# Layer 0 of a four-layer network as Strassen's seven products over both batch halves, with the input taken in four parts

## The chip, the cores and the metric

The kernel runs on one core of one Trainium2 chip. A core has a matrix engine (TensorE, PE in the profile), three engines for elementwise work (VectorE or DVE, ScalarE or ACT, GpSimd or POOL), and SyncE (SP), which here issues nearly all transfers between DRAM and the on-chip memory (SBUF). Matmul results land in PSUM, eight banks of 128 x 512 fp32, and another engine has to copy or add them out. The metric is device time in microseconds; lower is better. Every number is fp32 unless a tile is marked bf16.

## The reference

Four residual layers on a batch of 1024 images of 16 x 16 x 16. Ahead of each layer the activations are normalised in groups. Layer 0 is a tensor-train matrix of three cores; written out it is a dense 4096 x 4096 matrix applied to each image. Layers 1 and 3 are a neural cellular automaton (two depthwise convolutions, two dense layers, a mask), and layer 2 is a 3 x 3 convolution.

```python
def _L0_conv_ref(vector, core0, core1, core2):
    # IN_DIMS = OUT_DIMS = [16, 16, 16], RANKS = [1, 16, 16, 1], BATCH = 1024
    for core in cores:
        r, o, i, k = core.shape
        res_t = res.reshape(bs, r, i, -1)
        new = jnp.einsum('roik,brix->bkox', core, res_t)
        ...
    return res.reshape(bs0, *out_dims)
```

The tuned kernel doesn't apply the three cores one after another. It multiplies the cores into the 4096 x 4096 matrix on the chip, tile by tile, and multiplies that with the normalised activations. For each layer the result is x + layer(normalise(x)).

## The kernel before: the parts that matter

The batch is split into two chunks (n = 0, 1) of 512 images. `XN[n]` holds the normalised activations of one chunk in SBUF, 32 lines of 128 partitions x 512 images; `xf[l][n]` is the residual stream in DRAM. While TensorE works on one chunk, the other engines load and normalise the other one in the background.

The input is loaded with images on partitions, turned by TensorE, copied to `XN`, stored back to DRAM in the new order, and then normalised there with sums over all 32 lines:

```python
def input_steps(X, n):
    ...
    def turn(h, j, wh, xs):
        pt = psum([P, 4, P], "ptin")
        for bg in range(4):
            T.transpose(pt[:, bg], xs[bg][:, j, 8 * wh : 8 * wh + 8]..., ident)
        evac(X[:, 16 * wh + h + j], pt.rearrange("p g b -> p (g b)"))   # ACT and DVE in turn
    ...                                    # then 16 stores rows_in(xf[0][n], w) <- X

def norm_lines(X, gm, on_act=True):
    # sum over lines (DVE), mean over groups (one matmul with gm), subtract,
    # squares (ACT) and their sum (DVE), one matmul, rsqrt by Newton, multiply
    ...
```

Layer 0 is 32 output tiles x 32 input tiles for each chunk. The weight tiles of an output tile are built in two halves (`build`): eight matmuls of 16 rows, two to each of four 32-row groups of TensorE, into four PSUM banks, each copied to SBUF. For chunk 0 they are built and also saved to `w_dram`; for chunk 1 they are read back:

```python
def layer_train(X, n):
    ...
    def build(i, ih):
        wload(i, ih)                                   # the SBUF tile
        pw = [bank([P, 2, S, S], "w", "pw") for _ in range(4)]
        for v in range(2):
            for r in range(4):
                T.matmul(pw[r][:, v], g[32 * r : 32 * r + 16, ...], st["c0"][32 * r : 32 * r + 16],
                         start=True, stop=True)
        for r in range(4):
            evac(w[:, :, r].rearrange("p i v o -> p v i o"), pw[r])
        nc.sync.dma_start(w_dram[i, ih], ...)
    ...
    def piece(i, k):                                   # 32 output tiles x 8 pieces of 4 matmuls
        def go():
            if k == 0:
                st["po"] = bank([P, NB], "o", "po0")   # two banks
            for j in range(4 * k, 4 * k + 4):
                ih, i1 = divmod(j, S)
                T.matmul(po, st["w", i, ih][:, i1]..., X[:, 16 * ih + i1], start=j == 0, stop=j == NL - 1)   # L818
            prepare(i + 1, k)                          # build (n = 0) or load (n = 1) the next tile's weights
            if k == 0 and i + 1 < NL:
                fetch(i + 1)                           # the residual, 256 KB
            if k == 7:
                V.tensor_tensor(r, r, po, ALU.add)     # L827
                nc.sync.dma_start(tile_cw(xf[1][n], i), r)
```

The order of the program, up to the second layer:

```python
train_setup(X1)                                        # multiply cores 1 and 2 together, to g_dram
for step in input_steps(X0, 0) + norm_lines(X0, gm_in): ...   # chunk 0, nothing beside it
...
run(layer_train(X0, 0), (),
    [conv weights] + make1 + make3                     # weights of layers 1, 2 and 3
    + input_steps(X1, 1) + norm_lines(X1, gm_in))      # chunk 1, in the background
run(layer_train(X1, 1), [put(L1)] + load_cw(X0, xf[1][0]), norm_cw(X0, True), 0.2, by=0.15)
run(layer_nca(X0, 0, 1, L1), load_cw(X1, xf[1][1]), norm_cw(X1, False), 0.2, by=0.3)
```

`make1` and `make3` prepare the weights of the two automaton layers; their `fold` steps are matmuls of 9 x 36 x 512 (L370) whose results go to DRAM.

Of the kernel before, what the change touches and what calls it, by code (L numbers as in the profile page):

```python
# [9 lines left out]
F32 = mybir.dt.float32  # L10
# [5 lines left out]
ORDERED = {ENG.PE, ENG.DVE, ENG.Activation, ENG.Pool}  # L16
# [9 lines left out]
ALIVE = 0.1  # L26

# [72 lines left out]
def conv_preact_kernel(ctx: ExitStack, tc: tile.TileContext, a: dict, out: bass.AP):  # L100
# [15 lines left out]

    pool = {}
# [34 lines left out]
    def cst(name, shape, dt=F32):  # L152
# [3 lines left out]
    gind = cst("gind", [P, 2, 8])  # L156
    gm_in = cst("gm_in", [P, 8, 8, 2])
    V.tensor_reduce(gind[:, 0], ident.rearrange("p (w g i) -> p g w i", g=8, i=2), AX.XY, ALU.add)
    V.tensor_scalar(
        gm_in, gind[:, 0].unsqueeze(1).unsqueeze(3).broadcast_to([P, 8, 8, 2]), 1.0 / 512, None,  # L160
        ALU.mult,
    )
    gm_in = gm_in.rearrange("p w g i -> p (w g i)")
    gm_wc = cst("gm_wc", [P, 4, 8, 4])
    V.tensor_reduce(gind[:, 1], ident.rearrange("p (w g i) -> p g w i", g=8, i=4), AX.XY, ALU.add)
    V.tensor_scalar(
        gm_wc, gind[:, 1].unsqueeze(1).unsqueeze(3).broadcast_to([P, 4, 8, 4]), 1.0 / 512, None,
# [51 lines left out]
    def nca_weights(pre, room):  # L219
# [130 lines left out]
        def fold(n):  # L350
            def go():
                for f in range(2):

                    uses = []
                    for m, pats in enumerate(TRIPLES):
                        for i, pat in enumerate(pats):
                            over = m == 2 and i > 0 or m == 3 and i > 1
                            if over == bool(f):
                                for v in range(2):
                                    if pat[v] == n:  # L360
                                        ks = range(3) if m < 2 else [m - 2]
                                        uses += zip(ks, slots(m, i), [v] * 3)
                    if not uses:
                        continue
                    e = fold_e[f]
                    for a2 in range(2):
                        pe = psum([P, NB], pre + "pe")
                        for hh in range(2):
                            h0 = NB * (2 * hh + a2)
                            T.matmul(  # L370
                                pe[64 * hh : 64 * hh + 36], tp[:, n, f], fs[:, h0 : h0 + NB],
                                start=True, stop=True,
                            )
                        for hh in range(2):
                            rows = slice(64 * hh, 64 * hh + 36)
                            evac(e[rows, NB * a2 : NB * a2 + NB], pe[rows])
                    for k, s, v in uses:
                        for hh in range(2):
                            r0 = 64 * hh + 12 * k
                            nc.sync.dma_start(  # L380
                                wy.rearrange("q g v h s k -> v s (q g) h k")[
                                    v, s, :, 8 * hh : 8 * hh + 8
                                ],
                                e[r0 : r0 + 12].rearrange("p (h k) -> p h k", h=8),
                            )

            return go

        steps = [inputs, 8, dense0, 4, bias_lines, 4, bias_rows, dense1, xpats, taps, 8, order, 4]
        return L, steps + [x for n in range(len(TERMS)) for x in (fold(n), 10)]  # L390


# [44 lines left out]
    g_dram = dram.tile([S, 16, S, 256], F32, tag="g_dram", name="g_dram")  # L437
    w_dram = dram.tile([NL, 2, P, 16 * P], F32, tag="w_dram", name="w_dram")
    c_dram = dram.tile([16, 256], F32, tag="c_dram", name="c_dram")

    def train_setup(room):

        flat = room.rearrange("p n b -> p (n b)")
        c0 = flat[0:16, 14336:14592].rearrange("p (i o) -> p i o", o=S)
        c0n = flat[:, 0:32].rearrange("p (t k) -> p t k", t=2)
        c2 = flat[0:16, 512:768]
        c1n = flat[:, 1024:1536].rearrange("p (t f) -> p t f", t=2)
# [9 lines left out]
        c1t = flat[0:16, 2048:6144].rearrange("p (t i m) -> p t i m", t=2, i=S)  # L457
        for t in range(2):
            for i2 in range(0, S, 4):
                pt = psum([16, 4, P], "pc1")  # L460
                for j in range(4):
                    T.transpose(pt[:, j], c1n[:, t, 16 * (i2 + j) : 16 * (i2 + j) + 16], ident)
                evac(c1t[:, t, i2 : i2 + 4], pt)
        for t in range(2):

            g = flat[:, 6144 + 4096 * t : 10240 + 4096 * t].rearrange("p (o j i) -> p o j i", o=S, j=S)
            for i2 in range(0, S, 2):
                pg = psum([P, 2, S, S], "pg")
                for j in range(2):
                    T.matmul(pg[:, j], c1t[:, t, i2 + j], c2, start=True, stop=True)  # L470
                evac(g[:, :, i2 : i2 + 2, :].rearrange("p o j i -> p j o i"), pg)
            nc.sync.dma_start(
                g_dram[:, 8 * t : 8 * t + 8].rearrange("o k q f -> (k q) o f"),
                g.rearrange("p o j i -> p o (j i)"),
            )
        pt = psum([16, 2, P], "pc0")
        for t in range(2):
            T.transpose(pt[:, t], c0n[:, t], ident)
        for t in range(2):
            evac(  # L480
                c0[:, :, 8 * t : 8 * t + 8].rearrange("p i o -> p o i"),
                pt[:, t].rearrange("p (o i) -> p o i", i=S),
            )
        nc.sync.dma_start(c_dram, c0.rearrange("p i o -> p (i o)"))
# [70 lines left out]
    def rstd(st):  # L555


        def root():
            st["t"] = work([P, NB], "s", "t")
            A.activation(st["t"], st["ve"], AF.Sqrt)  # L560

        def newton():
            ve, t = st["ve"], st["t"]
            r = st["r"] = work([P, NB], "n", "r")
# [8 lines left out]
    def norm_lines(X, gm, on_act=True):  # L573
# [5 lines left out]
        def mean():  # L579
            st["p"] = psum([P, NB], "pmean")  # L580
            T.matmul(st["p"], gm, s1["s"], start=True, stop=True)

        def var():
            st["v"] = psum([P, NB], "pvar")
            T.matmul(st["v"], gm, s2["s"], start=True, stop=True)
# [9 lines left out]
    def norm_cw(X, on_act):  # L595


        st = {}
        sums, sq, mean, var, keep, spread = [], [], [], [], [], []
        for q in range(4):  # L600
# [4 lines left out]
            sums.append(more1)  # L605
            sq.append(each(X, l0, 8, lambda q=q: st["m", q], ALU.subtract) + more2)
# [13 lines left out]
            def keep_q(rows=rows):  # L620
                if rows.start == 0:
# [7 lines left out]
            mean.append(mean_q)  # L629
            var.append(var_q)  # L630
            keep.append(keep_q)
            spread.append(spread_q)
        steps = sums[0] + woven(sums[1], (2, mean[0]), (3, held(st, 0))) + [1] + sq[0]
        for q in (1, 2):
            steps += woven(
                sums[q + 1], (2, var[q - 1]), (3, mean[q]), (4, keep[q - 1]), (4, held(st, q))
# [3 lines left out]
        steps += woven(sq[2][4:], (2, mean[3]), (3, held(st, 3)))  # L640
        steps += woven(sq[3], (2, var[2]), (4, keep[2])) + [5, var[3], 2, keep[3]]
        steps += rstd(st) + [4, spread[0], 2, held(st, 0), 2]
        for q in range(4):
            mul = each(X, 8 * q, 8, lambda q=q: st["m", q], ALU.mult)
            steps += woven(mul, (2, spread[q + 1]), (3, held(st, q + 1))) if q < 3 else mul
# [32 lines left out]
    def input_steps(X, n):  # L678

        steps = []  # L680

        def load(h, xs):
            for bg in range(4):
                b0 = n * NB + bg * P
                x = work([P, 4, S, C], "xi", "xin")
                nc.sync.dma_start(
                    x.rearrange("p h w c -> p (h w c)"),
                    a["x"][b0 : b0 + P, h : h + 4].rearrange("b h w c -> b (h w c)"),
                )
                xs.append(x)  # L690

        def turn(h, j, wh, xs):
            pt = psum([P, 4, P], "ptin")
            for bg in range(4):
                T.transpose(  # L695
                    pt[:, bg], xs[bg][:, j, 8 * wh : 8 * wh + 8].rearrange("p w c -> p (w c)"), ident
                )
            evac(X[:, 16 * wh + h + j], pt.rearrange("p g b -> p (g b)"))

        for h in range(0, S, 4):  # L700
            xs = []
            steps += [lambda h=h, xs=xs: load(h, xs), 8]
            for j in range(4):
                for wh in range(2):
                    steps.append(lambda h=h, j=j, wh=wh, xs=xs: turn(h, j, wh, xs))
        for w in range(S):
            steps.append(
                lambda w=w: nc.sync.dma_start(  # L708
                    rows_in(xf[0][n], w),
                    X[16 * (w % 8) : 16 * (w % 8) + 16, 16 * (w // 8) : 16 * (w // 8) + 16],  # L710
                )
            )
# [515 lines left out]
```

## Time and profile before

| | |
|---|---|
| time, median of 3 | 3480.26 us (3471.43 to 3483.19) |
| span of the profiled execution | 3475.3 us |
| granted TensorE clock, mean | 0.968 |
| start to first product of layer 0 | 158.3 us |
| layer 0, chunk 0 and chunk 1 | 158.3 to 2102.9 us |
| moved by DMA | 441.76 MB, mean 127 GB/s |

How to read it: section 1 of the page gives each engine's busy time; section 2 cuts the span in 40 slices of about 87 us and prints the busy share of each in tenths. The chain that ended last is followed back from the final instruction, at each step to whatever released it; its shares by line say what the time was spent on. Groups of instructions are named by kernel line, engine, operation and tiles (L818 is the product of layer 0), with count, busy time and mean duration, and the idle time before them with its releaser. A matmul of this kernel leaves two records, and the ends of matmuls are modelled, so distances from start to start are used for its cost. A timeline lists instructions by start time and duration.

### The profile page before, as it was taken

The numbers are of one execution on the slowest core, as the hardware profiler recorded it, in microseconds if no ns is written. First come the engines' busy times: TensorE is split into PE (matmuls) and PEld (weight loads), VectorE is DVE, ScalarE is ACT, GpSimd is POOL, SyncE is SP. The second block draws the span as 40 slices with busy tenths as digits, with TensorE's granted clock in tenths as the row PEclk, the third lists the DMA queues.
The fourth block names the chain that finished last, engine by engine and source line by source line (L and its number), as shares of the span: only waits on it lengthen the run. The fifth ranks groups of instructions, "written<-read, shape, count | busy, mean of one in ns | idle before, by whom it ended". The sixth has DMA issues, their size and how long they took to land.

```text
span 3475.3 us, 35747 instructions
## 1 busy us (share of the span) xinstructions
PE 3310.1 (95%) x14298; PEld 1362.7 (39%) x14298; DVE 1272.4 (37%) x1400; ACT 883.6 (25%) x1370; POOL 420.1 (12%) x314
## 2 busy tenths in 40 slices
PE   5299999999999999999999999999999999999996
PEld 4144444444544444444444443333332333333332
DVE  5611111111135300111110013856777775855322
ACT  2201110111102000000000005666661115665553
POOL 0000000000000000000000002533550002532221
PEclk6599999999999999999999999999999999999998
DMA  8224323323382243222223224445446545442455
GB/s 227 68 89 121 100 88 109 99 89 139 137 181 94 102 157 115 103 91 91 91 91 106 93 76 159 131 129 174 139 127 229 197 157 174 131 130 80 140 148 182
DMA packets 202262, 441.76 MB, mean 127 GB/s; under 512 B 31986, under 2 KB 88222, under 8 KB 184158
## 3 DMA queue, kind: packets, MB, share of 16 engines
q1 hardware_dynamic: 202096, 439.47, 39.4%
q8 instruction: 113, 1.85, 0.2%
q14 instruction: 53, 0.43, 0.0%
HBM read 253.52 MB, written 174.19 MB: 123 GB/s over the span
## 4 chain that ended last, share of the span: by engine, by line
PE 84%; issue 5%; POOL 4%; DVE 3%; DMA 1%; SPq 1%; ACT 0%; POOLq 0%; DVEq 0%; ACTq 0%
PE po L818 51%; PE ph L1109 13%; PE po L962 5%; PE po L857 5%; PE po L877 2%; POOL res L1012 2%; PE pw L775 2%; POOL u L1011 2%; PE L_conv_pe L370 1%; DVE s L503 1%; DVE xn L532 1%; PE ptin L695 1%; PE pg L470 1%; SPq L708 1%; PE ptout L730 1%
## 5 line engine op out<-in xcount | busy, mean ns | idle before, releaser
L818 PE MATMUL po<-xn,w 128*128 128x512 f32 x4096 | 1801.2, 599 | 6.5 <-DMA w<-w_dram 6.5
L818 PEld LDWEIGHTS po<-xn,w 128*128 128x128 f32 x4096 | 775.7, 191 | 989.4 <-issue 989.3
L1112 ACT ACTIVATE hid<-ph,pack 128x512 f32<-128x512 f32 x1024 | 654.3, 687 | 459.2 <-PE ph L1109 332.8
L1109 PE MATMUL ph<-xn,wq 32*128 32x512 f32 x3664 | 574.0, 614 | 0.5 <-DMA wq<-L_conv_wy 0.5
L1011 POOL TENSOR_TENSOR u<-u,mask 128x512 f32<-128x512 f32 x128 | 195.8, 1530 | 2451.2 <-DMA nx<-xn 1573.9
L827 DVE TENSOR_TENSOR res<-res,po 128x512 f32<-128x512 f32 x64 | 44.0, 688 | 1002.6 <-PE po L818 1002.5
L1109 PEld LDWEIGHTS ph<-xn,wq 32*128 32x128 f32 x3664 | 229.2, 185 | 267.1 <-issue 237.1
L1109 PE MATMUL ph<-xn,pack 32*128 32x512 f32 x1288 | 297.0, 626 | 1.2 <-ACT hid L1112 0.9
L962 PE MATMUL po<-hid,pack 128*32 128x512 f32 x2048 | 280.2, 606 | 0.0
L532 DVE TENSOR_TENSOR xn<-xn,m 128x1024 f32<-128x1024 f32 x192 | 258.4, 1400 | 58.9 <-ACT m L543 41.6
L144 ACT COPY w<-pw 128x512 f32<-128x512 f32 x128 | 68.7, 589 | 713.0 <-PE pw L775 361.6
L146 DVE COPY w<-pw 128x512 f32<-128x512 f32 x128 | 82.5, 686 | 407.6 <-PE pw L775 313.6
L1012 POOL TENSOR_TENSOR res<-res,u 128x512 f32<-128x512 f32 x128 | 212.7, 1662 | 16.4 <-DMA res<-xf 6.7
L857 PE MATMUL po<-xn,convw 128*128 128x512 f32 x368 | 170.8, 608 | 8.3 <-DMA convw<-conv_dram 8.3
L974 DVE SCALAR_TENSOR_TENSOR u<-po,pack,xn 128x512 f32<-128x512 f32 x128 | 95.9, 749 | 178.4 <-PE po L962 174.9
L503 DVE TENSOR_TENSOR sq<-sq 128x1024 f32<-128x1024 f32 x108 | 146.6, 1358 | 24.2 <-ACT sq L517 19.6
L543 ACT COPY m<-pmean 128x512 f32<-128x512 f32 x20 | 11.7, 585 | 555.9 <-PE pmean L611 480.8
L1109 PEld LDWEIGHTS ph<-xn,pack 32*128 32x128 f32 x1288 | 113.0, 187 | 97.3 <-issue 66.7
L517 ACT ACTIVATE sq<-xn 128x1024 f32<-128x1024 f32 x80 | 84.5, 1057 | 253.2 <-DVE sq L503 185.9
L503 DVE TENSOR_TENSOR s<-s,xn 128x1024 f32<-128x1024 f32 x88 | 121.7, 1383 | 2.9
L962 PEld LDWEIGHTS po<-hid,pack 128*32 128x32 f32 x2048 | 42.4, 108 | 183.5 <-issue 134.9
L857 PEld LDWEIGHTS po<-xn,convw 128*128 128x128 f32 x368 | 67.3, 191 | 110.3 <-issue 93.8
(120 smaller groups left out, 1376.5 us busy)
## 6 DMA issues: line engine op xcount, KB each, us to landing
w_dram<-w SPq DMA_DIRECT2D x64, 1024.0 KB
res<-xf SPq DMA_DIRECT2D x256, 256.0 KB
w<-w_dram SPq DMA_DIRECT2D x64, 1024.0 KB
xf<-res SPq DMA_DIRECT2D x224, 256.0 KB
xn<-xf SPq DMA_DIRECT2D x96, 512.0 KB
wq<-L_conv_wy SPq DMA_DIRECT2D x192, 192.0 KB
xin<-in_x_dram SPq DMA_DIRECT2D x32, 512.0 KB
xf<-xn SPq DMA_DIRECT2D x32, 512.0 KB
```

The source lines that it names most:

```text
L146: V.tensor_copy(dst, src)
L503: return lambda: V.tensor_tensor(st["t"], st["t"], p(), ALU.add)
L517: A.activation(q, X[:, l : l + 2], AF.Square)
L532: V.tensor_tensor(part, part, m().unsqueeze(1).broadcast_to([P, 2, NB]), op)
L818: T.matmul(po, st["w", i, ih][:, i1].rearrange("p c v o -> p (c v o)"), X[:, 16 * ih + i1], start=j == 0, stop=j == NL - 1,)
L857: T.matmul(st["po", h][wh], conv["fw"][:, y], X[:, 16 * wh + h + y - 1], start=y == ys[0], stop=y == ys[-1],)
L962: T.matmul(po[32 * j : 32 * j + 32], nca["w1"][:, v], hid[j], start=v == 0, stop=v == 1)
L974: V.scalar_tensor_tensor(u, po, nca["b1"], X[:, 8 * q + w2], ALU.add, ALU.add)
L1011: G.tensor_tensor(u, u, st["m"][:, w2], ALU.mult)
L1012: G.tensor_tensor(r, r, u, ALU.add)
L1109: T.matmul(ph, w, x, start=k == 0, stop=k == len(tiles) - 1)
L1112: A.activation(h, ph, AF.Relu, bias=nca["bt"][:, r : r + 1])
```

## The change

Layer 0 is now one pass over both chunks. The two halves of the output (a2), two halves of a part of the input (b) and the two chunks (n) form 2 x 2 block matrices, and Strassen's scheme makes their product with seven block products in place of eight. The combinations of weights come for nothing extra in the weight build (core 0 is combined first, in `R`); those of activations are made by VectorE in place or in `E`; each product is added to or subtracted from one or two output blocks. The SBUF doesn't hold both chunks, so the input comes in four parts of 1024 values, and the output blocks are carried through DRAM from part to part. The first part is split further (phase 0: two products that need chunk 0 alone, phase 1: the other five), so that work starts while chunk 1 is being loaded.

```diff
+    PRODUCTS = [   # weight terms by output half, activation block, where the product goes
+        ({1: {0: 1, 1: 1}}, (0, 0), {(1, 0): 1, (1, 1): -1}),
+        ({1: {1: 1}}, (1, 0), {(0, 0): 1, (1, 0): 1}),
+        ({0: {0: 1, 1: 1}}, (1, 1), {(0, 1): 1, (0, 0): -1}),
+        ({0: {0: 1}}, (0, 1), {(0, 1): 1, (1, 1): 1}),
+        ({0: {0: 1}, 1: {1: 1}}, 0, {(0, 0): 1, (1, 1): 1}),
+        ({0: {0: -1}, 1: {0: 1}}, 1, {(1, 1): 1}),
+        ({0: {1: 1}, 1: {1: -1}}, 2, {(0, 0): 1}),
+    ]
...
+    def layer_train():
+        phases = [(0, 0, 2), (0, 2, 7), (1, 0, 7), (2, 0, 7), (3, 0, 7)]      # part, products from, to
+        units = [(ph, q, w) for ph in range(5) for q in range(4) for w in range(4)]
...
+        def build(u, v):
+            w, n = st["w", u], 4 * (m1 - m0)
+            pw = [bank([P, n, S], "w", "pw") for _ in range(4)]
             for r in range(4):
+                rows = slice(32 * r, 32 * r + 32)
+                T.matmul(pw[r], st["g", u][rows, v], st["R"][rows, p % 2, 64 * m0 : 64 * m1],
+                         start=True, stop=True)
+            for r in range(4):
+                A.copy(w[:, 0:n, 32 * r + 16 * v : 32 * r + 16 * v + 16], pw[r])
...
+        def piece(u, k):                                       # product k of unit u
+                po = bank([P, NB], "o", "po0")                 # three banks now
+                for t in range(4):
+                    x = E[:, what, t] if isinstance(what, int) else X[:, what[0], t, what[1]]
+                    T.matmul(po, st["w", u][:, 4 * k + t], x, start=t == 0, stop=t == 3)
+                if k == 0:
+                    build(u + 1, 0)
+                    if u > 0:
+                        store(u - 1)
+                if k == min(2, m1 - m0 - 1):
+                    build(u + 1, 1)
+                    gload(u + 2)
...                                                            # and fetch(u + 1); residual(u) at k = 1
+                gather(u, k, po, goes)                         # phase 0: A.copy; else V.tensor_tensor, one or two
```

The input's statistics are taken per image, before the turn, where a group's values lie along one partition; mean and 1/sigma are then turned to `mr`, and a part is normalised as it is loaded:

```diff
+        def stats(half, bg):
+            x = slots[:, 4 * half + bg].rearrange("p (q g i) -> p q g i", g=8, i=2)
+            for g in range(8):
+                V.bn_stats(st["b"][:, bg, g, half], x[:, :, g])
...
+        def turn(h, wh):      # as before, but evacuated by ACT alone; part 0 to SBUF, the rest by
+            ...               # three two-line buffers to xr[n] in DRAM
...
+    def part_steps(p):
+        steps = load_part(p) + [10] + normed(p, 0) + normed(p, 1)
+        return steps + combined(p, True) + combined(p, False)
```

The setup of the weights now works in `cores` and four `gs` steps that take their staging tile from the two `r` buffers, one of which holds the cores; each step ends with eight stores of 16 x 16 pieces of 512 bytes to `g_dram`. The order of SyncE is the program's throughout (`ENG.SP` in `ORDERED`). The new program order:

```diff
+        now(loads); now(setup); now(halves[0] + halves[1] + tail)       # shortened
+        start()
+        now(normed(0, 0, 1) + combined(0, True))
+        run(phases[0], bg: chunk 1's loads, statistics and turns, normed(0, 1), combined(0, False))
+        run(phases[1], bg: conv weights + make1 + make3 + part_steps(1))
+        for i in (2, 3):
+            run(phases[i], bg: part_steps(i))
+        run(phases[4] in four quarters, bg: statistics of the quarter before, scaling of quarters 0 to 2)
...
+        run(layer_nca(X0, 0, 1, L1), load_cw(X1, xf[1][1]), (last, 0.0, 0.18),
+            (norm_cw(X1, False), 0.21, 1.0), by=0.3)
```

In phase 4 the results of chunk 0 are gathered in `XN[0]` itself, where layer 1 reads them, so chunk 0 isn't loaded again; `last` is the normalisation of its last quarter, which layer 1 needs later than the others. `make1` and `make3` are cut into shorter steps, with one spare PSUM bank (m = 1) in place of two.

## The prediction

> **What bounds the kernel now.** I read the page's busy shares and its 40 slices first, then the chain that ended last, then the timeline of the first 160 us, and last the timeline of TensorE alone inside layer 0.
>
> ```profile
> PE 3310.1 (95%) x14298; PEld 1362.7 (39%) x14298; DVE 1272.4 (37%) x1400; ACT 883.6 (25%) x1370; POOL 420.1 (12%) x314
> ...
> PE   5299999999999999999999999999999999999996
> ...
> PE 84%; issue 5%; POOL 4%; DVE 3%; DMA 1%; SPq 1%; ACT 0%; POOLq 0%; DVEq 0%; ACTq 0%
> PE po L818 51%; PE ph L1109 13%; PE po L962 5%; PE po L857 5%; PE po L877 2%; POOL res L1012 2%; PE pw L775 2%; POOL u L1011 2%; PE L_conv_pe L370 1%; DVE s L503 1%; DVE xn L532 1%; PE ptin L695 1%; PE pg L470 1%; SPq L708 1%; PE ptout L730 1%
> ...
> L818 PE MATMUL po<-xn,w 128*128 128x512 f32 x4096 | 1801.2, 599 | 6.5 <-DMA w<-w_dram 6.5
> ```
>
> TensorE is full in every slice but the first two and the last, and half of the chain is one line: the products of layer 0 (L818). VectorE and ScalarE are below 40%. So outside the first two slices a microsecond off TensorE is a microsecond off the span, until another engine passes it.
>
> ```profile
> 2.27 9.08 SPq L686 DMA_DIRECT2D xin<-in_x_dram  x12
> ...
> 50.53 40.47 SPq L708 DMA_DIRECT2D xf<-xn  x16
> ...
> 52.29 17.96 DVE L503 TENSOR_TENSOR s<-s,xn 128x1024 f32<-128x1024 f32 x14
> ...
> 97.49 9.17 DVE L532 TENSOR_TENSOR xn<-xn,m 128x1024 f32<-128x1024 f32 x8 [11.00 <-DMA c<-c_dram]
> 106.58 19.83 DVE L503 TENSOR_TENSOR sq<-sq 128x1024 f32<-128x1024 f32 x15
> ...
> 136.78 18.26 DVE L532 TENSOR_TENSOR xn<-xn,r 128x1024 f32<-128x1024 f32 x16
> ...
> 158.28 5.64 PE L818 MATMUL po<-xn,w 128*128 128x512 f32 x8
> ```
>
> This is the start: load, then a serial chain of VectorE passes over the whole chunk (sum, subtract, squares, scale) with a store of 40.5 us in its middle. Layer 0 starts at 158.3 us.
>
> ```profile
> 304.19 1.15 PE L775 MATMUL pw<-c,gq 16*128 16x256 f32 x16
> 305.27 1.91 PE L370 MATMUL L_conv_pe<-xn 9*36 9x512 f32 x8
> 307.11 14.00 PE L818 MATMUL po<-xn,w 128*128 128x512 f32 x32
> 321.04 1.15 PE L775 MATMUL pw<-c,gq 16*128 16x256 f32 x16
> 322.11 7.13 PE L818 MATMUL po<-xn,w 128*128 128x512 f32 x16
> ```
>
> Columns are start and duration in us; the count is in records, two to a matmul (4096 records for the 2048 matmuls of L818). From start to start, 32 records take 321.04 - 307.11 = 13.93 us, so a matmul takes 0.87 us; where the granted clock is 1.00 (1812 to 1943 us: 304 records in 130.35 us) it is 0.86 us, which I use. A build of weights (8 matmuls, 16 records) occupies 1.08 us, a fold of the next layers' weights (4 matmuls) 1.84 us. Layer 0 runs from 158.3 to 2102.9 us, 1944.6 us: chunk 0 up to 1202 us with the builds in it (1044 us), chunk 1 895 us.
>
> **What the Trainium skill says.** (1) "TensorE: Matmul & The Clock Gate", Part 3: matmuls on different 32-row groups run at the same time. The trace agrees: the 8 build matmuls sit on four row groups; by columns each should take half of a 512-column matmul, 0.43 us, together 3.4 us, and they take 1.08. (2) "TensorEngine Tiling (Array Packing)", section PSUM Bottleneck: tiling does not speed up the emptying of PSUM. Agreed here: the bank copies L144 and L146 take 0.59 and 0.69 us, longer than their matmuls. (3) "DMA: Bandwidth & Descriptors", section Queues, rings and completion order: descriptors of a ring are consumed in ring order. The trace fits: the load of c issued behind the 16 stores holds VectorE until 97.5 us. (4) "TensorE: Matmul & The Clock Gate", Part 1: an idle TensorE falls to half clock; the windows from 60 to 160 us show 0.50. No page that I use states the cost of the new per-image statistics instruction.
>
> **The change part by part.**
>
> *Products.* Before, 32 output tiles x 32 input tiles x 2 chunks = 2048 matmuls. After, the 4096 inputs come in 4 parts; in each part 16 units make 7 products of 4 matmuls: 4 x 16 x 7 x 4 = 1792. 256 fewer x 0.86 = -220 us. They are on TensorE, which sets the end.
>
> *Building weights.* Before 64 builds x 1.08 = 69 us, once, kept in DRAM for chunk 1. After, 80 units x 2 builds = 160, and nothing kept. A build is 4 matmuls, one to a row group, with 448 columns for 7 products, 320 for 5 (phase 1), 128 for 2 (phase 0). If the four run together, the streaming is 0.86 x 448/512 = 0.75 us, 0.54 and 0.22; the old build has two rounds of 256 columns = 0.86 and takes 1.08, so a fixed 0.22 comes on top: 0.97, 0.76, 0.44. 96 x 0.97 + 32 x 0.76 + 32 x 0.44 = 93 + 24 + 14 = 131 us, +62.
>
> *Saved and reloaded weights.* 64 MB written and 64 MB read go, and with them the one wait at the chunk boundary, 6.5 us. In their place partial results travel (1 MB in and 1 MB out per unit of 26 us, plus 0.5 MB residual): about 100 GB/s, where the kernel before moves 127. Hidden.
>
> *Gathering.* 12 VectorE additions per unit of seven products x 0.69 us (L827) + one of 1.22 = 9.5 us in 26. The old kernel had 0.69 per 31 us. Normalising the next part adds 26 operations x 1.22 = 32 us per phase of 16 units. VectorE is then near 45%, with three PSUM banks between it and TensorE. ScalarE: 8 copies of 448 columns per unit, about 5 us in 26. Both off the path.
>
> *The start.* Loads as before (8 MB; the window from 10 to 20 us shows 397 GB/s), done near 25 us. Weight setup is now in four stages that share one free staging tile: each waits until the previous one's 1 MB has reached DRAM. With the coefficient tables' trip to DRAM ahead of them, stage stores start near 28 us and each takes about 10 us: the last stage is copied out of PSUM at about 60 us. VectorE is in order, so the 64 statistics instructions (256 elements, estimated at half of the 0.69 us of a 512-column copy: 0.35) run from 61 to 83 us. ScalarE copies 32 transposed lines (0.59 each) from 61 us, but three buffers tie it to the 8 MB of stores, which at 210 to 300 GB/s end near 100 us. Square root, Newton steps on 32 values, widening, transposes and copies: 8 us. Then 8 normalising operations and 2 combining ones x 1.22 = 12 us, of which the first product needs four. First product about 108 us, flow from about 112: against 158.3 that is -46 us.
>
> *New waits inside layer 0.* Phase 0 has to load, transpose and store chunk 1 within some 145 us (16 x (8 x 0.86 + 0.88) + 18 for the transposes), and its small weight loads queue behind 8 MB at about 390 GB/s, 22 us: I allow 12 us. Phase 1 (about 350 us) takes all weight preparation of layers 1 and 3 that was spread over 1044 us; waits of TensorE for small transfers (30 tap loads took 10.3 us to issue, 22 filter loads 16.3) and for the single spare PSUM bank: I allow 18 us. Four phase starts x 2.5 = 10 us. Together +40 us.
>
> *Moved.* The last quarter of the next normalisation goes into the NCA layer: three matmuls, 2.6 us, from one place of TensorE to another. Transposes of inputs are as many as before; the sums' matmuls of the input go (2), 16 small transposes come.
>
> Sum: 3480 - 220 + 62 - 6 - 46 + 40 = 3310 us, a gain of 170 (4.9%).
>
> **The rivals.** *A: the evacuation becomes the bound.* If VectorE or ScalarE falls behind, the three banks fill and TensorE stops at each product. For it: 12 additions in place of one, ordered engines, background operations of 1.22 us in bursts. Against it: 1.4 us of additions per product of 3.44 us. If every product lost 0.3 us, 448 x 0.3 = 134 us and the gain is gone: about 3440. *B: the builds do not overlap or their evacuation stalls TensorE.* If the 4 wide matmuls ran one after another, 160 builds would cost 96 x 3 + 32 x 2.2 + 32 x 0.9 = 387 us rather than 131: slower, about 3565. Against: the old build shows four groups at once; the new rows are at the same multiples of 32. *C: the transfers.* The manual order of SyncE means one store that waits holds the weight loads behind it. In phases 2 to 4 the loads are asked for more than a unit (26 us) ahead, which hides it; in phases 0 and 1 units last 8 and 19 us. At the worst 60 us more: 3370. *D: the start gains nothing*, when setup and statistics queue up in series to 150 us: 3350. *E: everything is hidden*, no new waits and start at 95 us: 3255.
>
> **Range and chances.** Products and builds are counted and timed, 10 us either way. The start carries 20, the waits 35. Range 3250 to 3380. Under 3411 us is faster by over 2%: that takes more than 100 us of waits beyond mine to miss: 0.91. Within 2%: 0.06. Slower: 0.03, rival B or a standstill in the queue.
>
> **What would show it.** Right: product records 3584, still 0.43 us apart; build records in runs of 8 lasting about 1.0 us at 28 tiles; first product near 110 us; phases 2, 3 and 4 about 16 x 26.0 = 416 us each (phase 4 some 10 more); VectorE busy by 40 to 50% there. Wrong: idle gaps of TensorE at every product (A), builds of 3 us (B), gaps released by weight loads or partial results in phases 0 and 1 (C), first product at 140 us or later (D).

## The result, and the profile after

The changed kernel takes 3389.62 us (median of 4, 3388.17 to 3390.83) against 3478.73 us (median of 4, one execution more than in the table above): a ratio of 0.9746, 95% interval 0.9728 to 0.9764. It is faster by 2.5%; 3310 us was predicted, with a range up to 3380.

From the page of the changed kernel, the lines that answer to those shown of before:

```profile
PE 3202.2 (94%) x14050; PEld 1270.3 (37%) x14050; DVE 1636.2 (48%) x2124; ACT 1066.5 (31%) x1944; POOL 420.0 (12%) x314
...
PE   5888797999999999999999999999999999999996
...
PEclk6999898999999999999999999999999999999998
...
L1026 PE MATMUL po<-xn,w 128*128 128x512 f32 x3584 | 1615.5, 606 | 15.9 <-ACT w L973 8.5
...
L968 PE MATMUL pw<-R,gq 32*128 32x448 f32 (+2 forms) x1280 | 143.9, 516 | 8.2 <-DMA gq<-g_dram 8.2
...
L371 PE MATMUL L_conv_pe<-xn 9*36 9x512 f32 x176 | 50.5, 652 | 50.8 <-DMA L_conv_wy<-xn 14.7
```

The products (L1026 now) are 3584 records, as counted. New are the slices 2 to 7 of the TensorE row: they read 8 8 8 7 9 7 where the old kernel had nines from the third on, and the clock row under them has eights. The fold matmuls (L371), 50.5 us of work, have as much idle time in front of them; before, it was 2.3 us. Two lines of before (the clock row, and the folds in the view of groups from 158 to 1170 us):

```profile
PEclk6599999999999999999999999999999999999998
...
L370 PE MATMUL L_conv_pe<-xn 9*36 9x512 f32 x176 | 45.9, 641 | 2.3 <-DVE xn L146 1.1 <-ACT xn L144 1.1
```

Where the 86 us between the two spans (3475.3 and 3388.9 us) come from, by the times at which stages start in the two timelines:

| stage | before | after | difference |
|---|---|---|---|
| start to first product | 158.3 | 93.6 | -64.7 |
| layer 0 | 1944.5 | 1911.1 | -33.4 |
| layers 1 to 3 | 1372.5 | 1384.2 | +11.7 |

Layer 0 by phases is 183.2, 450.4, 427.0, 421.7 and 428.9 us. Each engine's busy time in phases 0 to 4, in this order (columns: the stretch, its length, then busy time and records of each engine, granted clock, DMA share and GB/s):

```profile
93.60:276.80 183.20, 155.12 (x649) 71.95 (x649) 53.69 (x135) 59.71 (x195) 0.00 (x0) 0.97 0.39 144
276.80:727.20 450.40, 386.94 (x1097) 144.93 (x1097) 136.02 (x213) 79.90 (x192) 11.12 (x52) 0.91 0.34 96
727.20:1154.10 426.90, 423.74 (x1152) 178.13 (x1153) 187.08 (x248) 58.87 (x128) 0.00 (x0) 1.00 0.34 114
1154.10:1575.80 421.70, 421.70 (x1153) 177.59 (x1152) 173.56 (x234) 58.87 (x128) 0.00 (x0) 1.00 0.35 115
1575.80:2004.20 428.40, 428.40 (x1154) 179.04 (x1153) 183.45 (x248) 70.73 (x139) 0.00 (x0) 1.00 0.25 82
```

In phase 3 TensorE sets the pace: it is busy in all of its 421.7 us at full clock. Phase 1 makes five products per unit, not seven, and is longer than phase 3. TensorE is idle for 63 us of it, and its mean clock is 0.91. A clock of 0.5 or 1 with a mean of 0.91 over 450 us is half clock for some 81 us; the stretches of the trace at 0.50 add up to 85. What TensorE waited for in phase 1 (the view of waits; us in total, times, longest):

```profile
PE L_conv_pe L371 <- DMA L_conv_wy<-xn: 14.7, 1, 14.7
PE L_conv_pe L371 <- DMA xf<-r: 13.9, 1, 13.9
PE L_conv_pe L371 <- ACT xn L150: 13.0, 7, 3.0
PE L_conv_pe L371 <- DVE xn L152: 9.2, 6, 2.4
PE pw L968 <- DMA gq<-g_dram: 8.2, 1, 8.2
```

Two kinds stand out. Three long waits on transfers, two ahead of the first fold of a layer and one for a unit's weights, make 36.8 us. Thirteen short ones on copies out of PSUM make 22.2 us. One of the short ones, in the timeline (start, duration):

```profile
444.09 1.05 PE L371 MATMUL L_conv_pe<-xn 9*36 9x512 f32 x4
...
445.19 0.68 DVE L152 COPY xn<-L_conv_pe 36x512 f32<-36x512 f32 x1 [0.46 <-PE L_conv_pe L371]
445.95 0.58 ACT L150 COPY xn<-L_conv_pe 36x512 f32<-36x512 f32 x1 [0.36 <-ACT w L973]
446.58 1.05 PE L371 MATMUL L_conv_pe<-xn 9*36 9x512 f32 x4 [1.44 <-ACT xn L150]
```

Half a fold fills the only spare PSUM bank; the second half can't begin until VectorE and ScalarE have emptied it, one after the other. The Trainium skill says as much in "Trainium Kernel Development and Optimization", section Best Practices: regular bubbles can mean that a memory ran out. Here it is PSUM, and the bubbles are 1.4 us.

### The profile page after: what moved, and what is told of

Read it like the earlier page. It is cut to its first block, busy times and chain, and to the rows that moved or that the text cites. A ratio compares the mean times of both kernels' runs of the same rounds, so it can differ in the third digit from the quotient of the medians.

```text
span 3388.9 us, 37017 instructions
## 1 busy us (share of the span) xinstructions
PE 3202.2 (94%) x14050; PEld 1270.3 (37%) x14050; DVE 1636.2 (48%) x2124; ACT 1066.5 (31%) x1944; POOL 420.0 (12%) x314
## 4 chain that ended last, share of the span: by engine, by line
PE 68%; issue 7%; POOL 6%; DVE 2%; SPq 1%; DMA 1%; ACT 0%; POOLq 0%; DVEq 0%; ACTq 0%
PE po L1026 38%; PE ph L1351 12%; PE po L1099 5%; PE po L1204 4%; PE pw L968 3%; POOL res L1254 3%; POOL u L1253 3%; PE po L1119 2%; PE ptout L917 1%; PE L_conv_pe L371 1%; DVE xn L861 0%; PE ptx L1263 0%; PE pmean L670 0%; PE pvar L674 0%; DVE xn L152 0%
## 5 line engine op out<-in xcount | busy, mean ns | idle before, releaser
L1026 PE MATMUL po<-xn,w 128*128 128x512 f32 x3584 | 1615.5, 606 | 15.9 <-ACT w L973 8.5
L1026 PEld LDWEIGHTS po<-xn,w 128*128 128x128 f32 x3584 | 676.0, 193 | 910.0 <-issue 822.8
L1059 DVE TENSOR_TENSOR r<-r,po 128x512 f32<-128x512 f32 x576 | 378.1, 684 | 801.9 <-PE po L1026 725.0
L973 ACT COPY w<-pw 128x448 f32<-128x448 f32 (+2 forms) x640 | 246.8, 471 | 1356.6 <-PE pw L968 1356.0
L591 DVE TENSOR_TENSOR xn<-xn,m 128x1024 f32<-128x1024 f32 x160 | 222.3, 1438 | 30.6 <-ACT m L602 30.6
L1216 DVE SCALAR_TENSOR_TENSOR u<-po,pack,xn 128x512 f32<-128x512 f32 x128 | 95.8, 749 | 169.0 <-PE po L1204 161.6
L1351 PEld LDWEIGHTS ph<-xn,pack 32*128 32x128 f32 x1288 | 113.9, 187 | 103.2 <-issue 63.5
L968 PE MATMUL pw<-R,gq 32*128 32x448 f32 (+2 forms) x1280 | 143.9, 516 | 8.2 <-DMA gq<-g_dram 8.2
L1059 DVE TENSOR_TENSOR xn<-xn,po 128x512 f32<-128x512 f32 x96 | 64.4, 685 | 145.2 <-PE po L1026 145.2
L562 DVE TENSOR_TENSOR sq<-sq 128x1024 f32<-128x1024 f32 x78 | 109.8, 1407 | 15.4 <-ACT sq L576 12.3
L968 PEld LDWEIGHTS pw<-R,gq 32*128 32x128 f32 x1280 | 51.7, 185 | 128.6 <-issue 116.0
L371 PE MATMUL L_conv_pe<-xn 9*36 9x512 f32 x176 | 50.5, 652 | 50.8 <-DMA L_conv_wy<-xn 14.7
```

The lines of the kernel that those rows point to most:

```text
L562: return lambda: V.tensor_tensor(st["t"], st["t"], p(), ALU.add)
L591: V.tensor_tensor(part, part, m().unsqueeze(1).broadcast_to([P, 2, NB]), op)
L968: T.matmul(pw[r], st["g", u][rows, v], st["R"][rows, p % 2, 64 * m0 : 64 * m1], start=True, stop=True,)
L973: A.copy(w[:, 0:n, 32 * r + 16 * v : 32 * r + 16 * v + 16], pw[r])
L1026: T.matmul(po, st["w", u][:, 4 * k + t], x, start=t == 0, stop=t == 3)
L1059: V.tensor_tensor(r[at], r[at], po, ALU.add if sign > 0 else ALU.subtract)
```

## The experiments

All are edits of the changed kernel. Medians are of four runs; ratios are against the kernel before on the same chip.

### e1: two spare banks

```diff
-        stage(es, dict(gn, w=2, r=2, gq=2, R=1), dict(o=3, w=4, m=1))
+        stage(es, dict(gn, w=2, r=2, gq=2, R=1), dict(o=2, w=4, m=2))
```

> Edit: two PSUM banks for products and two spare ones, in place of three and one, in layer 0. Theory (the single spare bank makes TensorE wait between the two halves of a fold in phase 1 and between two turned lines in phase 0): the waits of 1.2 to 3 us go, 28 us of idle in phase 0 falls under 12, 26 us of short idle in phase 1 goes, and with it the half-clock stretches of 3.4 us behind it: 40 to 55 us faster than the changed kernel, about 3340 us. Rival (VectorE and ScalarE are what is late, and three product banks hide it): the waits only move to the products, with idle before them in phases 2 to 4: 3390 us or more.

Measured: 3333.11 us, ratio 0.9582 (0.9568 to 0.9597), 56.5 us under the changed kernel. Phase 0 falls from 183.2 to 164.4 us, phase 1 from 450.4 to 417.2. TensorE's waits in phase 1 of e1:

```profile
PE L_conv_pe L371 <- DMA L_conv_wy<-xn: 14.7, 1, 14.7
PE L_conv_pe L371 <- DMA xn<-L_conv_fz: 13.3, 1, 13.3
PE pw L968 <- DMA gq<-g_dram: 8.0, 1, 8.0
PE po L1026 <- DVE r L1059: 4.5, 2, 3.4
PE po L1026 <- DVE r L1057: 2.3, 1, 2.3
```

The short waits on copies are gone and the three long ones have stayed. The rival foresaw new waits of the products: there are some on VectorE now, but 6.8 us only, and phase 3 is 421.7 us as before. The third product bank bought little.

### e2: without the weight preparation of layer 3

```diff
-    L3, make3 = nca_weights("L3_conv_", X1[:, 16:32])
+    L3, make3 = L1, []
```

> Edit: the weights of layer 3 are not prepared, layer 3 takes those of layer 1 (this leaves work out). Theory (phase 1 is long because the whole weight preparation was pressed into it): phase 1 shrinks from 450 us by 20 us of folds, 15 us of the second wait before the first fold, half of the short waits and of the half-clock stretches, in all 60 to 70 us: about 3325 us. Rival (phase 1 is long because of its own gathering and partial results, and the preparation lies beside it): only the 20 us of fold matmuls and the other small ones go: about 3365 us.

Measured: 3290.17 us, ratio 0.946 (0.9443 to 0.9476), 99 us under the changed kernel, more than the theory gave. This kernel leaves out a part of the work, so its time is no target. Phase 1 is 356.0 us, 94 less. Its waits:

```profile
PE L_conv_pe L371 <- DMA gq<-g_dram: 9.8, 1, 9.8
PE pw L968 <- DMA gq<-g_dram: 8.1, 1, 8.1
PE po L1026 <- ACT w L973: 1.5, 1, 1.5
```

Not half of the thirteen short waits are gone, as I had expected, but all of them, with the single bank untouched. The two halves of a fold stand three units apart in the background list. That list has some 450 units in the changed kernel, 5.6 to a product of phase 1, so that both halves often fall behind the same product. Here it has some 260 over the same 80 products, 3.2 to one: the halves fall behind different products, and 3.4 us of matmuls lie between them. So the short waits need both: one bank, and steps that stand close.

### e3: the transfers in groups

```diff
-        steps = [inputs, 8, ..., xpats, taps, 8, order, 4]
+        steps = [inputs, 8, ..., xpats] + taps + [4, order] + blanks + [10]
+        # taps: 39 transfers in groups of 8, blanks: 8 in groups of 2, conv weights: 32 in groups of 6,
+        # with pauses of 4, 3 and 6 units after each group
```

> Edit: the same small transfers of the weight preparation, issued in groups of 2 to 8 with pauses between, and 10 units of pause ahead of the first fold; banks as in the changed kernel. Theory (bursts of 24 to 39 small transfers on SyncE hold back the weight loads and the first folds): the idle stretches of 13.9, 14.7, 8.2 and 2.2 us in phase 1 go, with some 20 us of half clock after them: 45 to 60 us faster, about 3338 us. Rival (transfers are late whatever their order, because the chain fz to fs to fold is long): stretches stay above 8 us each, under 15 us gained.

Measured: 3382.03 us, ratio 0.9724 (0.9709 to 0.9739). Only 7.6 us are gained, and by its total the theory would have fallen. The view of waits says otherwise:

```profile
PE L_conv_pe L378 <- ACT xn L150: 18.8, 10, 3.8
PE L_conv_pe L378 <- DVE xn L152: 15.9, 10, 2.4
PE L_conv_pt L265 <- DMA xn<-in_L_conv_fc_w_dram: 4.3, 1, 4.3
PE pw L980 <- DMA gq<-g_dram: 2.9, 1, 2.9
```

The 14.7, 13.9 and 8.2 us on transfers have become 2.9 (7.2 us for all transfers). But thirteen short waits of 22.2 us have become twenty of 34.7. The pauses take room in the list, the folds stand closer, and the bank waits rise. So the gain was paid back in part: TensorE idles for 45.2 us of phase 1 in place of 63.5, the phase is 14 us shorter (436.5 us), and phase 2 is 4 us longer (431.1 us), with one wait of 5.2 us for VectorE's combinations soon after its start.

That bursts of small transfers made the long waits can be seen in the trace of the changed kernel: SyncE needs from 336.9 to 350.0 us to issue the 39 loads of `taps`, GpSimd then puts them in order, and the first fold starts at 353.2 us. The edit also gave the first fold ten units of pause ahead of it; grouping and pause weren't tried apart.

### e4: the last quarter's squares on VectorE

```diff
+    nst, N = parts_cw(X0, False)
     last = alone(N, 3) + rstd(nst, slice(96, 128)) + [3] + scaled(N, [3])
```

> Edit: the last quarter's squares, which the change moved into layer 1, on VectorE in place of ScalarE. Theory (the first layer 1 stage grew by 8.3 us because the four squares of 1.06 us on ScalarE delay the evacuation of hidden lines at its start): the wait of 2.2 us and the half-clock stretch of 10.2 us behind it go, 4 to 6 us faster: about 3385 us. Rival (the growth is the three matmuls and VectorE's own work): within 1.5 us of the changed kernel.

Measured: 3387.35 us, ratio 0.9742 (0.9725 to 0.976), 2.3 us under the changed kernel, less than its own four executions differ (3385.87 to 3394.34). The first stage of layer 1 takes 270.1 us where it took 270.7 (262.3 before the change). The theory fell: the wait on ScalarE is gone, and one of 4.3 us ahead of the mask's matmuls has come.

### e5: e1, e3 and e4 together

> Edit: two spare banks, the small transfers in groups with pauses, and the last quarter's squares on VectorE, all three together. Theory (phase 1 loses to two things that trade places: pauses squeeze the folds together and the single spare bank then makes each of them wait; with two banks the pauses are free): phase 1 falls from 417 us (two banks alone) to 355 us, no idle stretch over 4 us is left in it: 60 us under the two banks alone, about 3272 us. Rival (the two edits remove the same time, so they don't add): 3325 us, as the two banks alone with the 8 us of the grouped transfers.

Measured: 3302.21 us (3294.37 to 3306.61), ratio 0.9495 (0.948 to 0.9509): 87 us under the changed kernel, where the three gains alone add up to 66, 2 of them within the noise (e4). They are worth more together, as the theory said, but it overstated by 30 us. Phase 1 is 381.4 us. Its waits and its stretch of time:

```profile
PE pw L980 <- DMA gq<-g_dram: 4.6, 2, 2.5
PE po L1038 <- DVE r L1071: 4.4, 1, 4.4
PE L_conv_pt L265 <- DMA xn<-in_L_conv_fc_w_dram: 3.9, 1, 3.9
```

```profile
256.80:638.20 381.40, 366.69 (x1097) 141.70 (x1097) 138.44 (x216) 79.71 (x192) 11.14 (x52) 0.97 0.40 113
```

No wait is over 4.4 us, and the clock is 0.97. With the same 1097 records TensorE is busy for 366.7 us instead of 386.9: 20 us of the old busy time came from the lower clock. This version beats both kernels.

### e6: the late setup stages moved back

```diff
-        now(setup)
-        now(halves[0] + halves[1] + tail)
+        now(setup[:3] + halves[0] + setup[3:4] + halves[1] + setup[4:] + tail)
```

> Edit: as e5, and the two setup stages whose weights are first needed in part 2 stand behind the statistics and turns of a half each. Theory (from 27 to 53 us the stages wait for their own stores in turn, at about 100 GB/s, while VectorE and ScalarE have nothing to do): first product at about 81 us in place of 93: 12 us under e5, about 3260 us. Rival (the start is bound by the 20 MB that it moves): first product at 88 us or later, 5 us or less.

Measured: 3312.78 us, ratio 0.9526 (0.9511 to 0.954), 10 us over e5. The first product comes at 95.8 us, where e5 had 92.4. By its number the rival holds (88 us or later), but its reason, the bytes moved, is not what the timeline of e6 shows: a moved stage stands in front of something that is needed.

```profile
76.06 7.19 PE L543 MATMUL pg<-cores,xn 16*128 16x256 f32 x16
...
83.29 0.69 DVE L152 COPY g<-pg 128x512 f32<-128x512 f32 x1 [2.67 <-PE pg L543]
83.90 2.43 DVE L824 BATCH_NORM_AGGREGATE small<-bn 128x2 f32<-128x12 f32 x32
```

The statistics are gathered at 83.9 us only, after VectorE has copied the last stage, whose 8 matmuls take 7.2 us (the granted clock is 0.50 from 76 to 84 us). That explains the 3.4 us at the start. Most of the rest lies elsewhere: the first stage of layer 1 takes 278.4 us where e5 has 270.4, with a wait of 4.8 us for the sums of the last quarter. The edit touches nothing there, and why that stage is longer stays open.

### e7: an eighth product

```diff
+                if ph > 1 and k == 6:
+                    again = bank([P, NB], "o", "po0")
+                    for t in range(4):
+                        T.matmul(again, st["w", u][:, 4 * k + t], E[:, what, t], start=t == 0, stop=t == 3)
```

> Edit: in the changed kernel, each of the 48 units of phases 2 to 4 makes its last product once more, into a bank that nobody reads. Theory (TensorE alone sets the pace there): 48 x 3.43 = 165 us more, about 3555 us. Rival A of the prediction (VectorE's additions set the pace): the extra matmuls lie beside them, under 60 us more.

Measured: 3553.74 us, ratio 1.0221 (1.0206 to 1.0236): 164.1 us more for 48 products, 3.42 us each. Nothing of a product is hidden: TensorE sets the pace of phases 2 to 4, and VectorE's additions lie beside it. So the product that the scheme saves is worth its full matmul time there, and rival A is out.

### e8: matmuls in the gaps

```diff
                 def half(a2, f=f, e=e):
+                    if a2 == 1:
+                        spare = bank([P, NB], "o", "po0")
+                        for t in range(2):
+                            T.matmul(spare, ident, part_tile(0)[0][:, 0, t, 0], start=t == 0, stop=t == 1)
```

> Edit: in the changed kernel two idle matmuls of 128 x 128 x 512 (1.7 us) stand between the two halves of each fold, where TensorE waits 1.4 us for the spare bank. Theory (the waits cost twice, because each is followed by 3.4 us or more of half clock): the half-clock stretches behind the short waits go, 10 to 20 us faster, although 22 x 1.7 us of work is added: about 3375 us. Rival (a wait costs its own length only): the filler takes the place of the waits and exceeds them a little, 0 to 15 us slower.

Measured: 3392.04 us, ratio 0.9759 (0.9743 to 0.9775), 2.4 us over the changed kernel. By the total the rival is right, and the gain I expected is not there. But phase 1 holds 38 us of added matmuls (22 x 1.72) and is only 4.6 us longer. Its idle time fell by 20 us (63.5 to 43.5), so some 13 us came back by the clock:

```profile
277.90:732.90 455.00, 411.51 (x1184) 155.32 (x1184) 136.10 (x213) 79.85 (x192) 11.12 (x52) 0.94 0.34 95
```

The clock is 0.94 in place of 0.91: half clock for 55 us, not 85. The stretches that are left lie at the three long waits; those behind short waits, 31 us in all, are gone. So the folds with their short waits did lower the clock, but what that cost is too little to pay for the filling. Whether the wait itself or the few rows of the folds lower it, e8 can't tell, since the filling adds work of 128 rows.

### e9: the list ended earlier

```diff
-                + make1 + make3 + part_steps(1), 0.0, 1.0,
+                + make1 + make3 + part_steps(1), 0.0, 0.95,
...
-            (last, 0.0, 0.18),
+            (last, 0.04, 0.2),
```

> Edit: two spare banks and grouped transfers as in e5; the background list of phase 1 ends at 95% of the phase, and the last quarter's normalisation starts at 4% of layer 1, with its squares on ScalarE as in the changed kernel. Theory (the 10 us of waits at the start of phase 2 come from normalising part 1 up to the very end of phase 1, and the first 4 us of waits of layer 1 from starting the last quarter at once): phase 2 falls from 428 to 421 us, the first layer 1 stage from 270 to 266 us: about 3290 us. Rival (the list squeezed into 95% makes the folds wait again by as much): within 4 us of e5, 3298 to 3306 us.

Measured: 3314.79 us, ratio 0.9531 (0.9513 to 0.9549), over e5 by 12.6 us. Phase 2 falls from 428.0 to 421.7 us as expected, but phase 1 grows from 381.4 to 399.4, and layer 1's first stage takes 272.3 us. A list squeezed into less of the phase costs more than it frees at its end. The total is beyond the rival's, and its mechanism isn't there: the folds wait for 2 us. The products wait for VectorE's additions, 11.2 us in place of 4.4:

```profile
PE po L1038 <- DVE r L1071: 7.9, 4, 3.1
...
PE po L1038 <- DVE r L1069: 3.3, 1, 3.3
```

VectorE is busy for 151.0 us of the phase, where e5 has 138.4: the normalisation of part 1, which ended in phase 2, now lies wholly here. What makes up the rest of the 18 us wasn't followed up.

## Why the prediction was wrong, point by point

**What was right.** TensorE bounds the kernel; 256 matmuls fewer are worth their full time (e7). A unit of seven products was put at 26.0 us and takes 26.36 (421.7 / 16): every stretch of products between builds has a small edge, and with 0.87 us per matmul, as the old kernel's stretches showed, it would have come out. The builds were put at 0.97 us; in the timeline the next product starts 0.96 us after one begins:

```profile
1052.23 1.03 PE L968 MATMUL pw<-R,gq 32*128 32x448 f32 x8
1053.19 7.13 PE L1026 MATMUL po<-xn,w 128*128 128x512 f32 x16
```

So the four row groups run together, as the old build suggested, and rival B is out. VectorE is busy for 173.6 of 421.7 us in phase 3 (41%; 45% was predicted).

**The start** was put at 46 us of gain, with a first product at 108; it gives 64.7, with the first at 93.6. The serial chain of setup stages was there: copies at 36 and 46 us behind the stores of the stage before, and at 54 us behind 7.2 us of matmuls, where I had the last at 60. The statistics take 21.0 us (22 estimated). The stores after that went faster than I allowed (the last is issued by 86 us; I had them end near 100).

**The step that failed** is the term "New waits inside layer 0", +40 us. Its mechanism, rival C and the single bank, was named, and its size was wrong. For phase 1 I had about 350 us of work and allowed 18 us of waits; it takes 450.4 us. Measured are 63 us of idle time. Another 55 us of busy time lie in stretches at half clock, which cost about half of that, 28 us (an estimate from the clock in the trace): 91 together. My sum has no term for the clock at all, although I had seen it at half in the start of the old kernel. Half of the weight preparation taken out shortens the phase by 94 us, of which the left-out matmuls are about 25 (e2); a second spare bank alone shortens it by 33 us (e1). For phase 0 I had some 145 us and allowed 12 us for loads that queue; it takes 183.2 us. Its idle time is 28 us, and most of it is the same single bank, 16.8 us of waits of turned lines on ScalarE's copies (5.0 us with two banks):

```profile
PE ptin L787 <- ACT lines L798: 12.9, 12, 1.3
...
PE ptin L787 <- ACT xn L790: 3.9, 4, 1.3
```

The two misses, 73 and 16 us, are more than the 80 us between prediction and result. The start gave 19 us more than predicted, and layers 1 to 3 took 12 us more than before.

What I missed in the reading: the bank copies and the issue times of small transfers stood in the old profile, and I wrote both down. In the old kernel they lay among 1044 us of products, here among 350. I priced each wait by a guess, and didn't ask how many steps fall behind one product: 450 units of background over 80 products are more than five to a product, so that both halves of a fold, three units apart, often come between the same two.

**Layers 1 to 3** were to stay equal but for 2.6 us that move there; they take 11.7 us more, 8.4 of it in the first stage of layer 1, where the last quarter's normalisation now lies. e4 and e9 moved parts of that and didn't win it back. In that stage TensorE is busy for 265.6 us in place of 258.4; three matmuls (2.6 us) are a part of that, and what the rest is made of stays open.

**The range** ended at 3380 because I gave the waits 35 us of leeway; they missed by 89. "Faster by over 2%" came true by half a per cent, and by luck: with the 46 us that I had predicted for the start, the time would have been about 3408 us, a gain of 2.0%.

## What to carry to other kernels

When a change shortens a bound stage, the background work that lay in it becomes denser: count background steps per step of the bound engine before and after, and ask of each shared buffer whether two users now meet between the same two steps. Two remedies for such a stage should be tried together, since each can move its gain to the other's wait (e3 alone 7.6 us; e1, e3 and e4 together 87). Ask which consumer waits in series before dividing spare banks: here giving up the third product bank cost 6.8 us of new waits, and with the second spare bank the kernel gained 56 us.

## What the runs showed of the hardware

A wait of TensorE among small matmuls can cost more than its length. The wait of 1.44 us that is shown above ended at 446.6 us; from 448.8 to 452.2 us the granted clock was 0.50 (stretches of the changed kernel, the clock is the third number from the end):

```profile
445.00:448.80 3.80, 2.36 (x9) 0.82 (x8) 1.36 (x2) 1.52 (x4) 0.00 (x0) 1.00 0.00 0
448.80:452.20 3.40, 3.40 (x5) 1.35 (x4) 0.00 (x0) 0.23 (x1) 0.00 (x0) 0.50 0.49 88
452.20:456.00 3.80, 3.80 (x11) 1.21 (x10) 1.37 (x2) 0.58 (x1) 0.00 (x0) 1.00 0.40 79
```

The Trainium skill, "TensorE: Matmul & The Clock Gate", section Why this matters for your kernels, asks to avoid idle gaps above about 3 us. In phase 1 shorter ones were enough. Of its thirteen short waits (0.97 to 2.96 us), among fold matmuls that use 9 rows of the array, eight were followed by a stretch at half clock within 2.3 us; two lie inside the stretches of the long waits, and three had none. Most of the waits of 1.2 to 1.3 us in phase 0, among products and transposes of 128 rows, left the clock at full (0.97 over the phase). A wait isn't even needed: in e5 a build and a whole fold (1.91 us from 434.6 us on) ran without any idle time, and a stretch at half clock followed:

```profile
430.40:437.20 6.80, 6.80 (x27) 2.46 (x26) 3.87 (x6) 1.99 (x5) 0.00 (x0) 1.00 0.34 104
437.20:440.60 3.40, 3.40 (x5) 1.35 (x4) 0.07 (x1) 0.58 (x1) 0.00 (x0) 0.50 0.40 73
```

It is the only stretch without a wait in that phase. So the length of the gap alone doesn't decide; whether the few rows of the folds do was not tried apart.
